# Two chained 2048-wide layers in fp32: a third Winograd level for product P5 in all but each phase's first group, where P2 stays whole; other places for the adapter rounds

## Chip, core, metric

One NeuronCore of a Trainium2 chip. The metric is the device time of one execution in microseconds, the median of several runs; the profile shows one further execution of the same program. TensorE (PE) multiplies, VectorE (DVE) adds and subtracts, ScalarE (ACT) copies from PSUM to SBUF, GpSimd (POOL) and SyncE (SP) issue DMAs.

## What is computed

The reference, cut to its core (x is 32 x 128 x 2048, all in fp32):

```python
base = einsum('bsi,oi->bso', x, weight) + bias
low = einsum('bsi,bri->bsr', x, lora_a[id0])        # rank 16, one of 8 adapters per batch
delta = einsum('bsr,bor->bso', low, lora_b[id0])
x = x + base + scale[id0][:, None, None] * delta    # first layer
x = x + einsum('bij,bkj->bik', x, weight1[id1])     # second layer: one of 16 weights per batch
```

The residual is folded into the weight: identity is added to the diagonal of W, so a layer is x (W^T + 1).

## The kernel before

**First layer.** It is Winograd's form of Strassen's product (7 products of half size in place of 8), nested. At the top level there are 7 **phases** (`PHASES`, L24): each names the quarters of x and of W whose signed sum is multiplied, where the result goes, and which products go down to the third level. A phase runs over 4 **groups** of batches, so there are 28 groups, n = 4i + g for phase i and group g. In a group the second level makes 7 products, P1 to P7, each a 512x512 piece of W with a 512x256 piece of x. A product that stays **whole** is 4 steps of 4 matmuls 128x256 (`whole`, L775). A product with a third level (**deep**) is 7 steps of 4 matmuls 128x128 (`third`, L799), on sums of its quarters that DVE makes first (`third_level`, L518: four operations of 256 elements for x, four of 512 for W) and adds up afterwards (`third_sums`, L816). Before the change P2, P3 and P4 are deep everywhere but for P2 of group 0; P1, P5, P6 and P7 are whole.

**Operands.** `total` in `a_tasks` and `w_tasks` adds up the loaded quarters of x and W (the tasks "x" and "w"), `inner` makes the second level's sums (S1 to S4 of x, T1, T2 and T4 of W; the tasks "s" and "t"), `third` the third level's ("x3" and "w3"). P5 multiplies S1 with T1, P6 S2 with T2, P3 S4 with W2, P4 A3 with T4.

**Memory.** All operands lie in one tile, `mem`. `Loads` (L112) hands its places out of pools: ten for x ("A", a group takes seven: four pieces, three sums), ten for W, six for staging ("st"), four for results ("z"). A load is issued on SP once a place is free, and the places come free as products end.

**Adapter.** Phase 1 (`LOW`, groups 4 to 7) loads all raw pieces of x and makes a @ x.T for the next group in four **rounds** (`lowrank`, L686: 32 small matmuls each, into a spare PSUM bank). Round q + 1 can start only when its staging loads have landed, and part of their places come free with round q. `lowrank_out` (L712) scales two rounds' result. In the last four phases ("final", groups 12 to 27) `add_low` (L736) makes low times b in two halves, with rows of b that `load_b` (L723) fetched on POOL's queue, and ACT copies the result (L759) to where `finish` (L840) adds it before the write to x1t in DRAM.

**Order.** Each engine works its queue off in order. PE's order is written out by hand in the loop over groups (L944 to L1067: `give` takes pairs of product and step, product 8 being P4 of the group before). DVE's order comes from `Plan` (L55): it keeps rough clocks of PE, DVE and DMA, and `fill` puts, wherever DVE's clock is behind PE's, the ready task with the smallest wanted time; `need` forces a task before the PE step that reads it. So a changed wanted time or estimated landing changes DVE's queue.

**Second layer** (L1075 on): 128 rounds of seven products each, DVE-heavy, weights streamed from DRAM. No line of it is touched.

Of the kernel before, what the change touches and what calls it, by code (L numbers as in the profile page):

```python
# [21 lines left out]
LOW = 1  # L22
KEPT = (2, 2)
PHASES = [  # L24
    ([(1, 0, 0)], [(1, 0, 0)], None, ((0, 0), (0, 1)), False, False, (2, 3, 4)),
# [3 lines left out]
        None, ((0, 1),), True, False, (2, 3, 4),  # L29
# [4 lines left out]
        (0, 1), ((1, 1), (1, 0)), False, False, (2, 3, 4),  # L34
# [4 lines left out]
        None, ((0, 1), (1, 1)), True, True, (2, 3, 4),  # L39
    ),  # L40
    ([(1, 0, 1)], [(1, 1, 0)], None, ((0, 0),), True, True, (2, 3, 4)),
# [3 lines left out]
        None, ((1, 0),), True, True, (2, 3, 4),  # L45
# [4 lines left out]
        None, ((0, 1),), True, True, (2, 3, 4),  # L50
# [61 lines left out]
class Loads:  # L112
# [13 lines left out]
    def pump(self):  # L126
        plan, full, rest = self.plan, set(), []
        for item in self.todo:
            key, pool, begin, behind, size = item
            if pool in full or not self.free[pool] or (behind and behind not in plan.did):  # L130
                full.add(pool)
                rest.append(item)
                continue
            slot = self.free[pool].pop(0)
            self.held[key] = (pool, slot)
            plan.did[key] = plan.pe
            if begin:
                begin(slot)
                plan.dma = max(plan.pe + 2.0, plan.dma) + size * 2.9
                plan.did[key] = plan.dma + 1.0  # L140
        self.todo = rest
# [20 lines left out]
def cond_resid_kernel(  # L162
# [13 lines left out]
):  # L176

# [187 lines left out]
    with tc.tile_pool(name="c0", bufs=1) as c0:  # L365
        L2 = 2 * NF

        more_w = {
            k: c0.tile([P, 3, 2, 2 * P], F32, tag=f"more_w{k}", name=f"more_w{k}") for k in (2, 3, 4)
        }  # L370
        more_a = {
            k: c0.tile([P, 3, 2, S], F32, tag=f"more_a{k}", name=f"more_a{k}") for k in (2, 3, 4)
        }

        low = c0.tile([P, B // 4, S], F32, tag="low", name="low")
        b_sel = c0.tile([P, 8, P], F32, tag="b_sel", name="b_sel")
# [3 lines left out]
        pairs_l = bank[:, 4:6], bank[:, 6:8]  # L380
        AT = {2: (0, 0), 3: (0, 1), 4: (1, 0), 1: (0, 0), 6: (0, 1), 7: (1, 0), 5: (1, 1)}
# [4 lines left out]
        def deep(n, k):  # L386

            return k in PHASES[groups[n][0]][6] and (n, k) != (0, 2)
# [4 lines left out]
                "W": (6, 0, 2, 8, 3, 5, 1, 9, 4, 7), "A": (25, 23, 28, 26, 27, 22, 21, 24, 29, 20), "z": (30, 31, 32, 33),  # L393
                "st": (36, 37, 39, 35, 34, 38), "k": (),
# [7 lines left out]
        def add_w(i, q):  # L402
# [14 lines left out]
            loads.add(("W", i, q), "W", lambda slot: load(slot, *terms[0][1:]), size=1.0)  # L417
# [96 lines left out]

        def signed(sign, dst, src):
            (add if sign > 0 else sub)(dst, dst, src)

        def third_level(work, m11, m12, m21, m22, more, of_x):  # L518

            s, u, v = (more[:, k] for k in range(3))  # L520
# [16 lines left out]
        def a_tasks(n, begin):  # L537
# [3 lines left out]
            forms = acts[n] = {k: {} for k in (2, 3, 4)}  # L541
# [4 lines left out]
            def total(q):  # L546
# [7 lines left out]
                if q == 0:  # L554
                    forms[1] = dst.rearrange("p (i n) -> p i n", i=4)
# [8 lines left out]
            def inner(k):  # L564
# [9 lines left out]
                if k < 4:  # L574
                    forms[4 + k] = dst.rearrange("p (i n) -> p i n", i=4)
# [8 lines left out]
            def third(k):  # L584
                src = slot(*{2: ("A", n, 1, 0), 3: ("S", n, 4), 4: ("A", n, 3, 0)}[k]).rearrange(
# [4 lines left out]
                    more_a[k], True,  # L590
                )

            for k, last_use, want in ((2, ("s", n, 4), 12), (3, ("s", n, 4), 32), (4, ("s", n, 1), 46)):
                if deep(n, k):
                    plan.add(
                        ("x3", n, k), begin + want, lambda k=k: third(k), last_use,
                        *([("PE", n - 1, k)] if n else []),
                    )

        def w_tasks(i, begin):  # L600
# [3 lines left out]
            forms = wts[i] = {k: {} for k in (2, 3, 4)}  # L604
# [4 lines left out]
            def total(q, f):  # L609
# [14 lines left out]
                if q == 0:  # L624
                    forms[1] = dst.rearrange("p (i n) -> p i n", i=4)
# [9 lines left out]
            def inner(k):  # L635
# [9 lines left out]
                if k < 4:  # L645
                    forms[4 + k] = dst.rearrange("p (i n) -> p i n", i=4)
# [8 lines left out]
            def third(k):  # L655
                src = view(*{2: ("W", i, 1), 3: ("W", i, 2), 4: ("T", i, 4)}[k]).rearrange(
# [7 lines left out]
            for k, last_use, want in ((2, 4, 9), (3, 3, 31), (4, 4, 45)):  # L664
                if k not in PHASES[i][6]:
                    continue
                plan.add(
                    ("w3", i, k), begin + want, lambda k=k: third(k), ("t", i, last_use),
                    *([("PE", 4 * i - 1, k)] if i else [("PE", 0, 2)] if k == 2 else []),
                )  # L670
# [15 lines left out]
        def lowrank(n, q, dst):  # L686
# [22 lines left out]
            plan.pe += 2.3  # L709
# [13 lines left out]
        def load_b(n):  # L723
            i, g = groups[n]
            r, c = PHASES[i][3][-1]
            for s in range(4):
# [3 lines left out]
                    in_=bt[ds(m, 1), c].rearrange("o r (k m) -> (o r) k m", k=8),  # L730
                )

        def low_banks(n):
            return pairs_a[1 - n % 2], pairs_l[3 * n % 2]

        def add_low(n, j):  # L736
# [3 lines left out]
            dst = low_banks(n)  # L740
            plan.pe += 1.3
            plan.need(("k", n, 0, j), ("k", n, 1, 1 - j))
            for k in range(4):
                for s in range(4):
                    nc.tensor.matmul(  # L745
                        dst[s // 2][:, s % 2, ts(k, S)], lhsT=b_sel[ts(s, RT), 4 * ((s // 2 + j) % 2) + k],
# [3 lines left out]
            low_out(n, j)  # L750

        def low_out(n, j):
            for t, src in enumerate(low_banks(n)):
# [3 lines left out]
                k = half(slot)  # L757
                for m in range(2):
                    nc.scalar.copy(k[:, ts(m, NF)], src[:, m])  # L759
# [14 lines left out]

        def whole(n, k, o):  # L775

            i = groups[n][0]
            pair = pairs_l[(3 * n + k) % 2] if k in (2, 3, 4) else pairs_a[(n + (k == 5)) % 2]
            dst = pair[:, o // 2, ts(o % 2, 2 * P)]
            if k in (2, 3, 4):  # L780
                w = mem[:, loads.slot({2: ("W", i, 1), 3: ("W", i, 2), 4: ("T", i, 4)}[k])]
                x = half(loads.slot({2: ("A", n, 1, 0), 3: ("S", n, 4), 4: ("A", n, 3, 0)}[k]))
                w, x = (v.rearrange("p (i n) -> p i n", i=4) for v in (w, x))
            else:
                w, x = wts[i][k], acts[n][k]
# [13 lines left out]
        def third(n, k, m):  # L799

            i, at = groups[n][0], 3 * n + k - 2
            pair, kept = pairs_l[at % 2], half(40 + at % 2)
            where = {2: (0, 0), 3: (0, 1), 5: (0, 1)}.get(m, (1, 0))
            dst = pair[:, where[0], ts(where[1], 2 * P)]
            w, x = wts[i][k][m], acts[n][k][m]
# [7 lines left out]
            if m in (1, 6, 7, 5):  # L813
                nc.scalar.copy(kept[:, ts((1, 6, 7, 5).index(m), 2 * P)], dst)  # L814

        def third_sums(n, k):  # L816
            at = 3 * n + k - 2
            pair, kept, z = pairs_l[at % 2], half(40 + at % 2), z_of(n, *AT[k])
            upper, c21, c22 = z[:, :NF], z[:, NF : NF + 2 * P], z[:, NF + 2 * P :]
            add(upper, upper, kept[:, :NF])  # L820
            add(upper, pair[:, 0], upper)
            add(c22, c22, kept[:, ts(2, 2 * P)])
            add(c22, c22, kept[:, ts(3, 2 * P)])
            add(c21, pair[:, 1, : 2 * P], c21)

        def ended(n, k):
# [3 lines left out]
            x, w, *last = {  # L830
                1: (("A", n, 0, 0), ("W", i, 0), 2, 3), 2: (("A", n, 1, 0), ("W", i, 1), 4),
                3: (("S", n, 4), ("W", i, 2), 2, 3), 4: (("A", n, 3, 0), ("T", i, 4), 1),
                5: (("S", n, 1), ("T", i, 1), 2), 6: (("S", n, 2), ("T", i, 2), 4),
                7: (("A", n, 2, 0), ("W", i, 3)),
            }[k]
            loads.done(x, *(("s", n, m) for m in last if (k, m) != (3, 2) and (k, m) != (3, 3)))
            if g == 3:
                loads.done(w, *(("t", i, m) for m in last))
# [24 lines left out]
        def result_tasks(n, begin):  # L863
# [10 lines left out]
            def single(k):  # L874
                if deep(n, k):
                    third_sums(n, k)
                else:
                    plain(*AT[k], pairs_l[(3 * n + k) % 2])

            plan.add(("third", n, 2), begin + 31, lambda: single(2), ("PE", n, 2))  # L880
            plan.add(("P5", n), begin + 40, both, ("PE", n, 5), ("PE", n, 6))
# [4 lines left out]
            plan.add(("third", n, 4), begin + 66, lambda: single(4), ("PE", n, 4))  # L886
# [34 lines left out]
        def give(n, *steps):  # L921

            for k, m in steps:
                of = n - 1 if k == 8 else n
                k = 4 if k == 8 else k
                if k not in (2, 3, 4):
# [7 lines left out]
        def ready(n, k):  # L934
# [3 lines left out]
            else:  # L938
                plan.need(*{
                    2: (("x", n, 1), ("w", i, 1, 1)), 3: (("s", n, 4), ("w", i, 2, 1)),  # L940
                    4: (("x", n, 3), ("t", i, 4)),
                }[k])

        for n, (i, g) in enumerate(groups):  # L944
# [10 lines left out]
            if lowering:  # L955
                plan.add(
                    ("out", n + 1, 0), begin + 33, lambda: lowrank_out(n + 1, 0, spare[:, 0, :S]),
# [3 lines left out]
                    ("out", n + 1, 1), begin + 46, lambda: lowrank_out(n + 1, 1, across[:, 0, :S]),  # L961
# [4 lines left out]
            if n:  # L966
                ready(n - 1, 4)
                plan.need(("third", n - 1, 2))
                if i == LOW:
                    plan.need(("out", n, 1))  # L970
# [6 lines left out]
            if final:  # L977
                plan.need(("P7", n - 1), ("third", n - 1, 3))
                add_low(n, 0)
                plan.fill()  # L980
            if n:
                give(n, (8, 3), (8, 4))
                ended(n - 1, 4)
            give(n, (1, 2), (1, 3))
            ended(n, 1)
            if ends:
                assert set(loads.free["W"]) == {0, 1, 2, 3}, loads.free
# [6 lines left out]
            if n == 0:  # L994
                give(n, *((2, o) for o in range(1, 5)))
            else:
                give(n, (2, 1))
            plan.need(("s", n, 1), ("t", i, 1))
            if n:
                give(n, (5, 0), (2, 2), (2, 6), (5, 1), (2, 5), (2, 7))  # L1000
            else:
                give(n, (5, 0), (5, 1))
            if lowering:
                if n:
                    plan.need(("third", n - 1, 4))
                lowrank(n + 1, 0, spare[:, 0, :S])
                plan.fill()
            if n:
# [214 lines left out]
```

## Time and profile before

| what | us |
|---|---|
| median of 3 runs (2959.79 to 2961.54) | 2960.71 |
| the profiled execution: its own time | 2960.55 |
| its span, first to last instruction | 2958.9 |
| first layer: PE from its first product to the second layer's first matmul (8.3 to 1408.3) | 1400.1 |
| second layer, from there to the end | 1550.6 |
| PE busy over the span (17,512 records, two for each matmul) | 2932.1 |
| DVE busy over the span | 2337.3 |
| DVE busy in 8.2 to 1408.3 | 893.4 |
| DVE busy in 1408.3 to the end | 1443.1 |
| ACT, POOL busy over the span | 340.5, 201.8 |

A row of the page's groups reads: line of the kernel, engine, operation, what is written from what, count, busy time and mean duration, then the idle time of the engine just before and what ended it. A line of the timeline gives start and length of a run of equal instructions, and in brackets the idle time before it with its releaser. The matmuls' lengths overlap, so a step's cost is the distance from its start to the next step's start.

### The profile page before, as it was taken

To read this page: it belongs to the slowest core of one execution; us is meant where nothing else is said; L and a number is where in the kernel's file an instruction comes from. 1 tells how busy PE (TensorE), PEld (TensorE's weight loads), DVE (VectorE), ACT (ScalarE), POOL (GpSimd) and SP (SyncE) were. 2 spreads that over 40 slices of the span, in tenths; PEclk is the share of its full clock that TensorE was granted. 3 is DMA by queue.
4 is the path that set the end of the run, shared out by engine and by line. 5 is a ranking of instruction groups with operands and counts; after the bars stand their busy time and mean duration, and the time that the engine had idled before them with its cause. 6 is when DMAs were issued, how large, how long until landed. Compare 5 with 4: busy or idle time off the path is not lost.

```text
span 2958.9 us, 43572 instructions
## 1 busy us (share of the span) xinstructions
PE 2932.1 (99%) x17512; PEld 1790.1 (60%) x17512; DVE 2337.3 (79%) x2168; ACT 340.5 (12%) x717; POOL 201.8 (7%) x323
## 2 busy tenths in 40 slices
PE   9999999999999999999999999999999999999999
PEld 8988899999989999999333333333333333333333
DVE  7457586685654745764999999999999999999997
ACT  1111111222222222222000000000000000000000
POOL 1122200111111111110000000000000000000000
PEclk9999999999999999999999999999999999999999
DMA  9498976778673635465999999999999999999995
GB/s 341 163 343 303 290 218 251 291 234 194 160 189 87 178 87 149 123 185 149 348 417 388 396 382 409 391 396 383 398 398 383 399 381 411 389 394 387 407 380 231
DMA packets 188713, 887.87 MB, mean 300 GB/s; under 512 B 21600, under 2 KB 21600, under 8 KB 122976
## 3 DMA queue, kind: packets, MB, share of 16 engines
q1 hardware_dynamic: 137616, 738.91, 63.5%
q0 software_dynamic: 32800, 113.28, 16.0%
q10 hardware_dynamic: 18096, 32.91, 3.4%
q8 instruction: 138, 2.26, 0.3%
q14 instruction: 63, 0.52, 0.0%
HBM read 754.98 MB, written 130.02 MB: 299 GB/s over the span
## 4 chain that ended last, share of the span: by engine, by line
PE 87%; DMA 5%; DVE 4%; issue 2%; SPq 0%; ACT 0%; POOL 0%; POOLq 0%; DVEq 0%; ACTq 0%
PE bank L1115 51%; PE bank L788 21%; PE bank L809 14%; DVE mem L282 2%; DMA mem<-in_xq_dram 2%; DVE mem L278 2%; DMA mem<-in_w0q_dram 1%; DMA x1t<-mem 1%; PE bank L745 1%; DMA mem<-in_w1q_dram 1%; PE bank L702 1%; DVE more_w L282 0%; SPq L444 0%; ACT mem L759 0%; DVE low L718 0%
## 5 line engine op out<-in xcount | busy, mean ns | idle before, releaser
L282 DVE TENSOR_TENSOR mem<-mem 128x2048 f32<-128x2048 f32 (+2 forms) x856 | 1494.5, 1773 | 147.9 <-DMA mem<-in_w0q_dram 44.5
L1115 PE MATMUL bank<-mem 128*64 128x512 f32 x5120 | 1122.9, 593 | 5.1 <-DVE u L278 2.9
L788 PE MATMUL bank<-mem 128*128 128x256 f32 x3616 | 835.5, 381 | 2.0 <-DVE low L718 1.6
L1115 PEld LDWEIGHTS bank<-mem 128*64 128x64 f32 x5120 | 367.8, 137 | 737.7 <-issue 696.7
L788 PEld LDWEIGHTS bank<-mem 128*128 128x128 f32 x3616 | 665.9, 191 | 82.9 <-DVE low L718 2.1
L278 DVE TENSOR_TENSOR mem<-mem 128x1024 f32<-128x1024 f32 (+2 forms) x441 | 347.5, 799 | 179.8 <-PE bank L809 75.0
L1115 PE MATMUL bank<-mem,s 128*64 128x512 f32 x2048 | 461.2, 592 | 0.0
L1115 PEld LDWEIGHTS bank<-mem,s 128*64 128x64 f32 x2048 | 147.1, 137 | 292.4 <-issue 289.2
L278 DVE TENSOR_TENSOR mem<-bank,mem 128x512 f32<-128x512 f32 (+2 forms) x195 | 127.5, 654 | 193.8 <-ACT mem L794 160.0
L809 PE MATMUL bank<-mem 128*128 128x128 f32 x1992 | 262.3, 277 | 4.3 <-ACT mem L759 4.1
L809 PEld LDWEIGHTS bank<-mem 128*128 128x128 f32 x1992 | 251.6, 192 | 17.0 <-ACT mem L759 6.2
L794 ACT COPY mem<-bank 128x512 f32<-128x512 f32 x224 | 131.5, 587 | 640.9 <-PE bank L788 635.8
L1121 ACT COPY pv<-bank 128x512 f32<-128x512 f32 x32 | 18.8, 586 | 1518.6 <-PE bank L1115 944.0
L855 POOL DMA_DIRECT2D x1t<-mem x160 | 118.1, 759 | 978.2 <-DVE mem L278 377.1
L809 PE MATMUL bank<-more_a,more_w 128*128 128x128 f32 x1328 | 171.8, 276 | 4.2 <-DVE more_w L282 3.2
L809 PEld LDWEIGHTS bank<-more_a,more_w 128*128 128x128 f32 x1328 | 166.6, 193 | 8.9 <-issue 4.7
L814 ACT COPY mem<-bank 128x256 f32<-128x256 f32 x332 | 124.4, 375 | 380.1 <-PE bank L809 373.6
L278 DVE TENSOR_TENSOR pv<-bank,pv 128x512 f32<-128x512 f32 x64 | 44.2, 691 | 66.7 <-PE bank L1115 65.4
L278 DVE TENSOR_TENSOR mem<-mem,ident 128x1024 f32<-128x1024 f32 (+1 forms) x84 | 85.4, 1029 | 11.1 <-DMA mem<-in_w1q_dram 10.8
L809 PE MATMUL bank<-more_a,mem 128*128 128x128 f32 x664 | 89.2, 277 | 0.0
L809 PEld LDWEIGHTS bank<-more_a,mem 128*128 128x128 f32 x664 | 84.9, 191 | 4.7
L809 PE MATMUL bank<-mem,more_w 128*128 128x128 f32 x664 | 87.7, 275 | 0.0
(43 smaller groups left out, 686.9 us busy)
## 6 DMA issues: line engine op xcount, KB each, us to landing
mem<-in_w1q_dram SPq DMA_DIRECT2D x512, 1024.0 KB, 10.9
mem<-in_xq_dram SPq DMA_DIRECT2D x192, 512.0 KB, 7.2
x1t<-mem POOLq DMA_DIRECT2D x160, 512.0 KB, 7.8
mem<-in_w0q_dram SPq DMA_DIRECT2D x88, 512.0 KB, 10.2
mem<-x1t SPq DMA_DIRECT2D x80, 512.0 KB, 9.0
out_dram<-res ACTq DMA_DIRECT2D x124, 256.0 KB, 7.4
mem<-in_at_dram POOLq DMA_DIRECT2D x64, 128.0 KB, 5.5
xsum<-mem POOLq DMA_DIRECT2D x16, 512.0 KB, 7.3
```

What stands on the lines that cost most here:

```text
L278: nc.vector.tensor_tensor(dst, a, b, ALU.add)
L282: nc.vector.tensor_tensor(dst, a, b, ALU.subtract)
L702: nc.tensor.matmul(dst[ts(2 * r + s, RT)], lhsT=a_sel[:, 2 * r + s, k, i], rhs=raw[r, k][:, i, s], start=(h == k == i == 0), stop=(h == k ...
L745: nc.tensor.matmul(dst[s // 2][:, s % 2, ts(k, S)], lhsT=b_sel[ts(s, RT), 4 * ((s // 2 + j) % 2) + k], rhs=low[ts(s, RT), 4 * r + g], star ...
L788: nc.tensor.matmul(dst, lhsT=w[:, m, ts(o, P)], rhs=x[:, m], start=(k < 6 and o % 2 == 0 and m == 0), stop=(m == 3), skip_group_check=True,)
L794: nc.scalar.copy(by_block(z_of(n, *AT[k]))[:, o - 1 : o + 1], pair[:, o // 2].rearrange("p (k t m) -> p k t m", k=2, t=2),)
L809: nc.tensor.matmul(dst[:, ts(o, P)], lhsT=w[:, f, ts(o, P)], rhs=x[:, f], start=(m in (1, 2) and o == f == 0), stop=(f == 1), skip_group_c ...
L814: nc.scalar.copy(kept[:, ts((1, 6, 7, 5).index(m), 2 * P)], dst)
L855: nc.gpsimd.dma_start(out=of_x1t(rc, g, t, j), in_=src.rearrange("p (s x) -> p s x", s=2), accum_op=ALU.add if adding else ALU.bypass,)
L1115: nc.tensor.matmul(dst[ts(j, M)], lhsT=xts[pair, k4 // 2][k][:, j, k4 % 2 * 2 + i], rhs=w1s[n][k][:, j, i], start=(k4 == 0 and i == 0), st ...
L1121: nc.scalar.copy(pv[:, 0], dst)
```

## The change

P5 is added to every phase's list of deep products; `deep` now leaves P2 and P5 whole in each phase's first group (g = 0). The other edits: x's third-level sums share three buffers that go round (`more_x`) in place of one per product; one of the ten "A" places (half 28 of `mem`) and one new buffer become W's third-level sums for P5; rows of b are held by halves and fetched twice per final group; the third-level sums of W for P2 and P5 wait for the first group's whole product, since they overwrite part of W; P2's and P5's steps are interleaved in a new order; the four rounds of a @ x.T stand elsewhere; the waits for `lowrank_out` move; `Plan` takes a load to land 4 us later than it did. In the second layer nothing changes.

```diff
-    ([(1, 0, 0)], [(1, 0, 0)], None, ((0, 0), (0, 1)), False, False, (2, 3, 4)),
+    ([(1, 0, 0)], [(1, 0, 0)], None, ((0, 0), (0, 1)), False, False, (2, 3, 4, 5)),
...
-                plan.did[key] = plan.dma + 1.0
+                plan.did[key] = plan.dma + 5.0
...
-        more_w = {
-            k: c0.tile([P, 3, 2, 2 * P], F32, tag=f"more_w{k}", name=f"more_w{k}") for k in (2, 3, 4)
-        }
-        more_a = {
-            k: c0.tile([P, 3, 2, S], F32, tag=f"more_a{k}", name=f"more_a{k}") for k in (2, 3, 4)
-        }
+        w_c0 = c0.tile([P, 10, 2, 2 * P], F32, tag="more_w", name="more_w")
+        w_mem = mem[:, 14, :L2].rearrange("p (k i n) -> p k i n", k=2, i=2)
+        more_w = {k: [w_c0[:, 3 * m + n] for n in range(3)] for m, k in enumerate((2, 3, 4))}
+        more_w[5] = [w_mem[:, 0], w_mem[:, 1], w_c0[:, 9]]
+        more_x = c0.tile([P, 3, 3, 2, S], F32, tag="more_x", name="more_x")
+        kept_5 = c0.tile([P, 2 * P], F32, tag="kept_5", name="kept_5")
...
-        b_sel = c0.tile([P, 8, P], F32, tag="b_sel", name="b_sel")
+        b_sel = c0.tile([P, 4, P], F32, tag="b_sel", name="b_sel")
...
+        SMALL = (2, 5, 3, 4)
...
-            return k in PHASES[groups[n][0]][6] and (n, k) != (0, 2)
+            i, g = groups[n]
+            return k in PHASES[i][6] and (g > 0 or k in (3, 4))
...
-                "W": (6, 0, 2, 8, 3, 5, 1, 9, 4, 7), "A": (25, 23, 28, 26, 27, 22, 21, 24, 29, 20), "z": (30, 31, 32, 33),
+                "W": (6, 0, 1, 8, 2, 5, 3, 9, 4, 7), "A": (20, 21, 27, 29, 24, 25, 26, 22, 23), "z": (30, 31, 32, 33),
...
-            loads.add(("W", i, q), "W", lambda slot: load(slot, *terms[0][1:]), size=1.0)
+            loads.add(
+                ("W", i, q), "W", lambda slot: load(slot, *terms[0][1:]), size=1.0,
+                behind=("A", 4 * i - 3 + q, 3, 0) if i == LOW + 1 and q < 3 else None,
+            )
...
-            for k, last_use, want in ((2, ("s", n, 4), 12), (3, ("s", n, 4), 32), (4, ("s", n, 1), 46)):
+            for k, last_use, want in ((2, 4, 12), (5, 2, 12.5), (3, 4, 32), (4, 1, 46)):
                 if deep(n, k):
+                    before = turn(n, k) - 3
+                    before = [("PE", before // 4, SMALL[before % 4])] if before >= 0 else []
...
-            for k, last_use, want in ((2, 4, 9), (3, 3, 31), (4, 4, 45)):
-                if k not in PHASES[i][6]:
-                    continue
-                plan.add(
-                    ("w3", i, k), begin + want, lambda k=k: third(k), ("t", i, last_use),
-                    *([("PE", 4 * i - 1, k)] if i else [("PE", 0, 2)] if k == 2 else []),
-                )
+            for k, last_use, want in ((2, 4, 50), (5, 2, 51), (3, 3, 31), (4, 4, 45)):
+                if k in PHASES[i][6]:
+                    before = ("PE", 4 * i - 1, k) if deep(4 * i, k) else ("PE", 4 * i, k)
...
...
+                upper, third_one, fifth = kept_of(n, k)
+                to = {1: upper[:, : 2 * P], 6: upper[:, 2 * P :], 7: third_one, 5: fifth}[m]
+                nc.scalar.copy(to, dst)
+            elif m == 4 and k == 5:
+                nc.scalar.copy(z_of(n, 1, 1)[:, NF : NF + 2 * P], dst)
...
+            if k != 5:
+                add(upper, upper, first)
+                add(c22, c22, third_one)
+                add(c21, pair[:, 1, : 2 * P], c21)
             add(upper, pair[:, 0], upper)
+            add(c22, c22, fifth)
...
-            plan.add(("P5", n), begin + 40, both, ("PE", n, 5), ("PE", n, 6))
+            plan.add(("third", n, 5), begin + 26.5, lambda: single(5), ("PE", n, 5))
+            plan.add(("P5", n), begin + 40, both, ("third", n, 5), ("PE", n, 6))
...
-                if i == LOW:
-                    plan.need(("out", n, 1))
                 give(n, (8, 1))
...
                 add_low(n, 0)
+                load_b(n, 1)
...
+            if i == LOW:
+                plan.need(("out", n, 1))
             give(n, (1, 2), (1, 3))
...
-                give(n, (5, 0), (2, 2), (2, 6), (5, 1), (2, 5), (2, 7))
...
-                lowrank(n + 1, 0, spare[:, 0, :S])
...
-                give(n, (5, 2), (2, 3), (2, 4), (5, 3))
...
-                lowrank(n + 1, 1, spare[:, 0, :S])
+                give(n, (2, 1), (2, 2))
+                ready(n, 5)
+                give(n, (5, 1), (2, 6))
+                if not deep(n, 2):
+                    give(n, (5, 2), (2, 3))
+                if lowering:
+                    plan.need(("third", n - 1, 4))
+                    lowrank(n + 1, 0, spare[:, 0, :S])
+                    plan.fill()
+                give(n, *[(5, 2)] * deep(n, 2), (2, 5), (5, 6), *[(5, 3)] * (not deep(n, 2)))
+                give(n, (2, 7), (5, 5), *[(2, 3)] * deep(n, 2), (5, 7), (2, 4))
+                give(n, *[(5, 3)] * deep(n, 2), (5, 4))
...
-            give(n, *((6, o) for o in range(4)))
+            give(n, (6, 0))
+            if lowering:
+                lowrank(n + 1, 1, spare[:, 0, :S])
+                plan.fill()
+            give(n, *((6, o) for o in range(1, 4)))
...
-            if lowering:
-                lowrank(n + 1, 2, across[:, 0, :S])
...
-                give(n, (7, 0), (3, 6), (3, 5), (7, 1))
+                give(n, (7, 0))
                 if lowering:
-                    lowrank(n + 1, 3, across[:, 0, :S])
+                    plan.need(("third", n, 5))
+                    lowrank(n + 1, 2, across[:, 1, :S])
                     plan.fill()
-                give(n, (3, 7), (7, 2), (3, 3), (3, 4), (7, 3))
+                give(n, (3, 6), (3, 5), (7, 1), (3, 7), (7, 2), (3, 3), (3, 4))
+                if lowering:
+                    lowrank(n + 1, 3, across[:, 1, :S])
+                    plan.fill()
+                give(n, (7, 3))
```

## Prediction

> **What bounds the kernel.** I read the table of windows first, split where the second layer's first matmul starts, then the page's chain.
>
> ```profile
> 8.20:1408.30 1400.10, 1385.05 (x10312) 1268.98 (x10312) 893.40 (x1296) 320.42 (x684) 196.53 (x310) 1.00 0.68 207
> 1408.30:2958.90 1550.60, 1540.67 (x7169) 514.93 (x7168) 1443.10 (x871) 18.76 (x32) 1.72 (x2) 1.00 0.97 385
> PE 87%; DMA 5%; DVE 4%; issue 2%; SPq 0%; ACT 0%; POOL 0%; POOLq 0%; DVEq 0%; ACTq 0%
> ```
>
> Behind each stretch's length stand the busy times of PE, PEld, DVE, ACT and POOL, the granted clock and the DMA share. In the first layer PE works 1385 of 1400 us and DVE 893: PE sets the end, and time changes only with PE's steps or its waits. The second layer, 1550.6 us, keeps its instructions and, by the order of the changed program, its first loads wait for the same products; I leave it as it is.
>
> The timeline of PE gives the steps' prices:
>
> ```profile
> 58.29 1.06 PE L809 MATMUL bank<-more_a,mem 128*128 128x128 f32 x8
> 59.19 1.06 PE L809 MATMUL bank<-mem,more_w 128*128 128x128 f32 x8
> 60.08 3.62 PE L788 MATMUL bank<-mem 128*128 128x256 f32 x16
> 63.53 1.05 PE L809 MATMUL bank<-mem 128*128 128x128 f32 x8
> ```
>
> From start to start a deep step takes 0.89 us (median 0.893 over the layer), a whole step 3.45/2 = 1.726. The waits of PE in this layer:
>
> ```profile
> PE bank L702 <- DMA mem<-in_xq_dram: 4.9, 5, 2.0
> PE bank L809 <- ACT mem L759: 4.1, 3, 3.0
> PE bank L809 <- DVE more_w L282: 3.2, 1, 3.2
> PE bank L788 <- DVE low L718: 1.6, 3, 0.7
> PE bank L809 <- DVE more_a L282: 1.0, 1, 1.0
> PE bank L788 <- DVE mem L278: 0.4, 1, 0.4
> ```
>
> They cost more than their sum. Adding up by how much each step exceeds its usual length gives 24.7 us: 1.2 at 38 us; 4.1 in a @ x.T at the end of group 3; 9.8 in group 4, the first of phase 1; 2.7 in groups 5 to 7; 6.9 in the final groups (4.9 of it at group 16). The rest is half clock:
>
> ```profile
> 217.87 1.05 PE L809 MATMUL bank<-mem 128*128 128x128 f32 x8
> 222.11 2.04 PE L809 MATMUL bank<-more_a,more_w 128*128 128x128 f32 x8 [3.19 <-DVE more_w L282]
> 223.95 2.55 PE L788 MATMUL bank<-mem 128*128 128x256 f32 x8
> 226.34 1.05 PE L809 MATMUL bank<-more_a,more_w 128*128 128x128 f32 x8
> 221.90:225.30 3.40, 3.19 (x12) 2.95 (x13) 3.23 (x7) 0.37 (x1) 0.00 (x0) 0.50 1.02 417
> ```
>
> After 3.19 us idle the clock is 0.50 for 3.4 us; the deep step takes 1.84 in place of 0.89, the whole one 2.39 in place of 1.73: 1.6 us on top.
>
> **PE's steps.** Before, 3 x 28 - 1 = 83 products are deep; after, P3 and P4 in 28 groups and P2 and P5 in 21: 98. Fifteen more (21 P5 gained, 6 P2 lost). A whole product is 4 x 1.726 = 6.90 us, a deep one 7 x 0.893 = 6.25: 15 x 0.65 = **-9.8 us**. [...] The row says 0.52 of a whole step, over 581 steps with weight loads: I take the row.
>
> **DVE.** A deep P5 adds four operations of 0.42 (more_a, 128x256) and sums of 0.69 and 0.42: 2.8 us a group; each phase adds four of 0.69 for W; six P2 give back about 3 each. In 650:700 DVE is busy 28.7 of 50 us, so this lies beside PE where its place in the queue is early enough. In the changed order of a usual group, DVE makes P2's and P5's x sums behind P7's, P3's and one result's additions; they are queued to end some 11 us after the last P7 step starts, and the first step that reads one starts at 19. Cover 8 us; each us beyond costs PE one.
>
> **ACT.** P5 goes from two copies of 0.59 to five of 0.375, and between a copied step and the step that overwrites its bank there are now at least two deep steps, 1.8 us. Before, P4 has a single step (0.89) there and PE shows no wait for L814. Nothing.
>
> **POOL and DMA.** 64 more b fetches, four per final group, about 1 us each on POOL (0.5 busy, 0.5 issue; POOL is busy some 20 of 200 us). The second half's fetch waits for add_low's matmuls, and behind it on POOL stands the write of result (0,1), later by some 5 us; its reader, the copy after the second add_low, comes 20 us later. Nothing, 0 to 3. Nine x places in place of ten: a group's last x pieces load after P1 and P2 (16 and 26 us in) and are read 10 us and more later, at 7.2 us per landing (the page's x row). Nothing, 0 to 4.
>
> **Waits that go.** At 38 us PE waited for P3's x sums because DVE did the scale table first; now the sums come first: 1.2 to 0. The half of `low` that held PE at group starts (1.6) is asked for four steps and more later: 0. The rounds of a @ x.T: each needs loads issued when the round before has freed its staging. The distances were 5.2, 6.9 and 7.0 us of PE work, now 10.7, 8.7 and 7.9 (6.9 between the first two in group 4), against 7.2 to land. I take 4.1 to 0.5 in group 3, and 2.7 to 1.5 in groups 5 to 7.
>
> **The wait that stays: group 4.** Here DVE is full (44.3 of 50 us in 200:250). The fourth round has moved from mid P3 to just before P7's last step, so DVE work moves behind it too: its x sum, four `low` operations, and the last W sum, whose staging load is issued only after the round. In the trace of before:
>
> ```profile
> 195.61 1.63 SPq L423 DMA_DIRECT2D mem<-in_w0q_dram  x2
> 202.60 1.23 DVE L278 TENSOR_TENSOR mem<-mem 128x1024 f32<-128x1024 f32 x1 [0.39 <-DMA mem<-in_w0q_dram]
> ```
>
> Some 7 us from the first issue to DVE's release. Then DVE's queue: that W sum 1.2, P7 1.2, P3's additions 2.6, four x sums 4.9, P4's additions 2.6, T1 2.3 = 14.8, so T1 is there 21.5 us after the round. PE's first P5 step comes after 5 whole steps, 7 deep and 2 whole: 7 x 1.73 + 7 x 0.89 = 18.4. Wait 3.2, plus 1.6 of half clock as at 222 us. [...] From T1 to `low` DVE has T2, T4, T3 6.9, two x third levels 3.4, three of W 8.2, two x roundings 4.9, P2's addition 1.2, `low` 1.6 = 26.2; PE to its reader, P3's second step, 10 whole steps, two rounds at 1.88, one deep step and the half clock: 17.3 + 3.8 + 0.9 + 1.6 = 23.6. Wait 2.6. Group 4: 9.8 to 7.4. Between: 4 if the load lands faster, 13 if it lands like the page's 10.2 us for W.
>
> **Final groups.** Group 16 waited 3.0 us for ACT's L759 copy, itself held by a write to x1t. In the new order a W piece is loaded ahead of that stretch and the other result's writes go later; I take 4.9 to 1.5, and 2.0 for the other groups' (unchanged). Bounds 0.5 and 7.
>
> **Sum.** Waits after: 0 + 0.5 + 7.4 + 1.5 + 3.5 = 12.9; for 21 groups of new interleaving that no row shows I add 2: 15. Change -9.8 - 24.7 + 15 = -19.5; on the profiled execution's own 2960.55 (span 2958.9 and 1.65 around it; the median of the runs is 2960.71) **2941 us**.
>
> **Rivals.**
> - The waits only move (chance 0.2): DVE and DMA around phase 1 are as full as before, each gap closed opens the next, and 21 to 25 us of waits stay. For it: the load-bound DVE queue of group 4. Against: the rounds' wider distances. Only PE's steps remain: 2960.6 - 9.8 = 2951.
> - Slower (0.06): x's late places. S4's place now comes free only when P3 of the group before ends, so S4 and P2's third level start behind it, in every group. If x loads or DVE's backlog eat the 8 us of cover, PE waits in all 27 later groups. It decides from 9.8 + 9.7 = 19.5 us, 0.7 a group; with 1 us, 27 more than my sum: 2968. Against: DVE's idle third.
> - The level does not pay (0.03): deep steps spaced wider when P2 and P5 alternate, by 0.06 us or more each; 147 P5 steps x 0.067 eat the 9.8: 2951. Against: all 581 deep steps show one spacing whatever stands beside them.
>
> **Chances.** 0.71 for the forecast (own range 2934 to 2948). What a measurement here can tell from no change is 0.2%, 5.9 us: faster means below 2954.8. The first and third rivals lie on the faster side, with about a fifth of them within; faster 0.87, within 0.06, slower 0.07. The range, with 4 to 13 at group 4, 0.5 to 7 in the final groups and the moving-waits case: 2931 to 2953.
>
> **What would show it.** Deep matmul records 4648 to 5488, whole ones 3616 to 3136; PE's first layer 1380 us; no wait of L809 for more_w at group 4's P2, but one of L806 for DVE's `mem` sum at its P5, followed by clock 0.50; waits for in_xq_dram under 2 us. Wrong if PE shows waits at each group's P2 or P5, or if ACT's copies hold PE there.

## The result, and the profile after

| | before | after |
|---|---|---|
| median of 6 runs each, us | 2960.25 (2958.6 to 2964.58) | 2938.43 (2936.55 to 2939.1) |
| ratio after / before, 95% interval | | 0.9923 [0.991, 0.9936] |
| profiled execution: own time, span, us | 2960.55, 2958.9 | 2939.1, 2937.5 |
| first layer of the profile, us | 1400.1 | 1378.3 |
| steps' excess in it (waits, half clock), us | 24.7 | 12.6 |

The kernel is 0.77% faster, 21.8 us by the medians. The forecast of 2941 missed by 2.6 us. First the windows of the changed kernel, split where the second layer's first matmul starts (length of the stretch, then busy times of PE, PEld, DVE, ACT and POOL, the granted clock, DMA's share), then the first line of the page's chain:

```profile
8.20:1386.50 1378.30, 1367.48 (x10674) 1266.89 (x10674) 934.96 (x1401) 325.38 (x723) 230.34 (x374) 1.00 0.70 210
1386.50:2937.50 1551.00, 1540.47 (x7169) 508.59 (x7168) 1442.82 (x871) 18.75 (x32) 1.71 (x2) 1.00 0.97 385
PE 91%; DMA 3%; DVE 3%; issue 2%; SPq 0%; POOL 0%; ACT 0%; POOLq 0%; DVEq 0%; ACTq 0%
```

All of the gain lies in the first layer: 21.8 us there, while the second takes 1551.0 in place of 1550.6. DVE does 42 us more in the first layer (935 for 893) and PE still ends it. The waits of PE up to 1420 us, by what ended them (us in total, times, longest):

```profile
PE bank L717 <- DVE mem L279: 3.0, 2, 1.8
...
PE bank L806 <- DVE mem L283: 2.3, 1, 2.3
PE bank L826 <- DVE low L733: 2.3, 1, 2.3
...
PE bank L717 <- DMA mem<-in_xq_dram: 1.5, 1, 1.5
...
```

L806 is a whole step, L826 a deep one, L717 a round of a @ x.T. The 4.9 us in front of the rounds for x's loads have become 1.5, the waits for `more_w` and for half of `low` at group starts are gone. New is the first row: in groups 5 and 6 the first round waits for additions of DVE. PE's timeline shows four of these places:

```profile
213.95 5.45 PE L806 MATMUL bank<-mem 128*128 128x256 f32 x24 [2.34 <-DVE mem L283]
...
238.84 1.16 PE L826 MATMUL bank<-mem 128*128 128x128 f32 x8 [2.30 <-DVE low L733]
...
244.44 1.08 PE L717 MATMUL bank<-mem 128*32 128x128 f32 x32 [1.49 <-DMA mem<-in_xq_dram]
...
275.41 1.84 PE L717 MATMUL bank<-mem 128*32 128x128 f32 x58 [1.23 <-DVE mem L279]
```

The first is P5's first step in group 4, waiting for T1; the second is P3's second step there, waiting for `low`; the next is in the middle of the third round, still in group 4, waiting for a load of x; the last is the first round in group 5. The clock did not fall after any of them: the trace grants 1.00 throughout the first layer, where the kernel before had four stretches at 0.50.

### The profile page after: what moved, and what is told of

It is laid out like the page before. It is cut to its first block, busy times and chain, and to the rows that moved or that the text cites. A ratio compares the mean times of both kernels' runs of the same rounds, so it can differ in the third digit from the quotient of the medians.

```text
span 2937.5 us, 44863 instructions
## 1 busy us (share of the span) xinstructions
PE 2913.5 (99%) x17872; PEld 1780.8 (61%) x17872; DVE 2378.7 (81%) x2274; ACT 345.4 (12%) x756; POOL 235.6 (8%) x387
## 4 chain that ended last, share of the span: by engine, by line
PE 91%; DMA 3%; DVE 3%; issue 2%; SPq 0%; POOL 0%; ACT 0%; POOLq 0%; DVEq 0%; ACTq 0%
PE bank L1140 51%; PE bank L806 20%; PE bank L826 18%; DVE mem L279 1%; DVE mem L283 1%; PE bank L760 1%; DMA x1t<-mem 1%; DMA mem<-in_w1q_dram 1%; PE bank L717 1%; DMA mem<-in_w0q_dram 1%; DMA mem<-in_xq_dram 0%; DMA id_sb<-in_id_dram 0%; DVE low L733 0%; DVE more_x L283 0%; SPq L429 0%
## 5 line engine op out<-in xcount | busy, mean ns | idle before, releaser
L283 DVE TENSOR_TENSOR mem<-mem 128x2048 f32<-128x2048 f32 (+3 forms) x892 | 1514.3, 1725 | 208.6 <-PE bank L826 101.3
L806 PE MATMUL bank<-mem 128*128 128x256 f32 x3136 | 715.4, 380 | 4.8 <-DVE mem L283 2.3
L806 PEld LDWEIGHTS bank<-mem 128*128 128x128 f32 x3136 | 578.7, 190 | 77.8 <-DVE mem L283 2.7
L279 DVE TENSOR_TENSOR mem<-mem 128x256 f32<-128x256 f32 (+2 forms) x423 | 331.5, 810 | 74.8 <-ACT mem L812 38.7
L826 PE MATMUL bank<-mem 128*128 128x128 f32 x2352 | 301.3, 276 | 2.6 <-DVE low L733 2.3
L826 PEld LDWEIGHTS bank<-mem 128*128 128x128 f32 x2352 | 289.3, 192 | 11.9 <-DVE low L733 2.5
L279 DVE TENSOR_TENSOR mem<-bank,mem 128x256 f32<-128x256 f32 (+2 forms) x210 | 135.5, 676 | 169.1 <-PE bank L826 92.6
L826 PE MATMUL bank<-more_x,more_w 128*128 128x128 f32 x1232 | 158.6, 275 | 0.0
L826 PEld LDWEIGHTS bank<-more_x,more_w 128*128 128x128 f32 x1232 | 151.7, 192 | 3.5 <-issue 0.8
L826 PE MATMUL bank<-more_x,mem 128*128 128x128 f32 x1120 | 146.1, 276 | 0.0
L826 PEld LDWEIGHTS bank<-more_x,mem 128*128 128x128 f32 x1120 | 136.6, 192 | 3.3
L826 PE MATMUL bank<-mem,more_w 128*128 128x128 f32 x784 | 103.7, 275 | 0.0
```

The source lines that it names most:

```text
L279: nc.vector.tensor_tensor(dst, a, b, ALU.add)
L283: nc.vector.tensor_tensor(dst, a, b, ALU.subtract)
L806: nc.tensor.matmul(dst, lhsT=w[:, m, ts(o, P)], rhs=x[:, m], start=(k < 6 and o % 2 == 0 and m == 0), stop=(m == 3), skip_group_check=True,)
L826: nc.tensor.matmul(dst[:, ts(o, P)], lhsT=w[:, f, ts(o, P)], rhs=x[:, f], start=(m in (1, 2) and o == f == 0), stop=(f == 1), skip_group_c ...
```

## Experiments

Each kernel was timed beside the kernel before on the same chip. Since that kernel's median differed from chip to chip (2961.0, 2963.5, 2961.5), ratios are what to compare. "First layer" and "excess" are read from the profile as in the table above: PE's time from the first product to the second layer, and the sum of what steps take beyond their usual length. "Second layer" is the rest of the profiled execution. No line of it differs between these kernels, and it still varies by 8 us, so a gain in the first layer is not yet a gain of the whole.

| run | ratio [95% interval] | first layer, us | excess, us | second layer, us |
|---|---|---|---|---|
| before | 1 | 1400.1 | 24.7 | 1550.6 |
| after | 0.9923 [0.991, 0.9936] | 1378.3 | 12.6 | 1551.0 |
| p5_whole | 0.9949 [0.9936, 0.9963] | 1385.3 | 6.7 | 1548.8 |
| rounds_alone | 0.9996 [0.9988, 1.0004] | 1396.0 | 20.6 | 1554.7 |
| nine_places | 0.9988 [0.998, 0.9997] | 1398.4 | 23.9 | 1548.1 |
| p2_first | 0.9928 [0.9914, 0.9941] | 1378.1 | 16.8 | 1552.0 |
| rounds_p2 | 0.9995 [0.9986, 1.0004] | 1398.1 | 19.3 | 1556.4 |
| p5_not01 | 0.9916 [0.9902, 0.9929] | 1374.2 | 5.3 | 1553.1 |
| p5_not1 | 0.9927 [0.9913, 0.994] | 1380.4 | 13.0 | 1549.7 |
| landing_1 | 0.9941 [0.9928, 0.9955] | 1384.5 | 19.5 | 1551.3 |
| rounds_p2_land | 1.0004 [0.9995, 1.0013] | 1399.3 | 20.6 | 1553.1 |
| rounds_back | 0.995 [0.9937, 0.9964] | 1386.7 | 21.8 | 1549.8 |
| late_p2 | 0.9916 [0.9903, 0.993] | 1375.5 | 9.9 | 1550.8 |
| late_p25 | 0.991 [0.9895, 0.9925] | 1377.0 | 14.7 | 1550.9 |

**P5's third level undone.** In the changed kernel:

```diff
-    ([(1, 0, 0)], [(1, 0, 0)], None, ((0, 0), (0, 1)), False, False, (2, 3, 4, 5)),
+    ([(1, 0, 0)], [(1, 0, 0)], None, ((0, 0), (0, 1)), False, False, (2, 3, 4)),
...
```

and so in all seven phases.

> The changed kernel with P5 whole in every group (its third level undone; P2 whole in each phase's first group, and rounds, needs and places as changed). It has 21 products P5 more as four whole steps in place of seven deep ones: 21 x (4 x 1.726 - 7 x 0.893) = 21 x 0.65 = 13.7 us more of steps. Theory (the third level of P5 pays its steps in full, and the waits went for the other reasons): 2938.4 + 13.7 = 2952, and 1 to 3 us less than that if the wait at P5's first step in group 4 came with P5's deep form. Rival (the third level does not pay; all of the gain is from waits): 2938 to 2941.

Measured: 2945.58 us, 0.9949. The step sum is there (first layer less excess: 1378.6 for 1365.7, so 12.9 us), but the waits fall with it from 12.6 to 6.7. Neither theory named that size: P5's level is worth 7 us net, 12.9 of steps less 5.9 of waits that come with it. Of the gain of 22 us, 15 stand without it, although P2 in six groups is slower there than before.

**The rounds alone, in the kernel before.**

```diff
-            if lowering:
-                lowrank(n + 1, 1, spare[:, 0, :S])
-                plan.fill()
...
-            give(n, *((6, o) for o in range(4)))
+            give(n, (6, 0))
+            if lowering:
+                lowrank(n + 1, 1, spare[:, 0, :S])
+                plan.fill()
+            give(n, *((6, o) for o in range(1, 4)))
```

and likewise for the third and fourth round and `low`'s second half.

> The kernel before with the four a @ x.T rounds at their new steps, the other half of the bank and the need for low's second half two steps later; no third level for P5, all places as before. Theory (the rounds' waits were real and go): group 3's 4.1 us fall to about 0.5, groups 5 to 7's 2.7 us to about 1.5, and a part of group 4's 9.8: 2952 to 2956. Rival (waits only move to the next need): 2959.5 to 2961.

Measured: 2959.3 us, 0.9996, no change that can be told. In the rounds the reasoning holds: group 3's 4.1 us are gone, and groups 5 to 7 show no wait at all. But group 4 goes from 9.8 to 14.5. Its waits (us in total, times, longest):

```profile
PE bank L788 <- DVE mem L282: 6.2, 1, 6.2
...
PE bank L809 <- DVE low L718: 2.0, 1, 2.0
```

PE comes to P5's first step earlier and waits there 6.2 us for T1, then 2.0 for `low`. The first layer is 4.1 us shorter all the same, and the second takes it back: it is 4.1 us longer. SP issues its next loads of weights from 1422.31 us on, behind a write to x1t (1409.16 in the kernel before), DVE waits for such a load, and PE for DVE; the eight records behind that wait take 3.63 us, where eight such records of the changed kernel take 1.92 at a clock of 1.00 (from 1427.19 us on):

```profile
1422.31 31.51 SPq L312 DMA_DIRECT2D mem<-in_w1q_dram  x17
```

```profile
1437.04 3.63 PE L1118 MATMUL bank<-mem,s 128*64 128x512 f32 x8 [3.99 <-DVE mem L282]
```

So the rival (waits only move) holds for this part taken alone: in part they move to group 4, in part beyond the layer. Which place in memory held the loads is not shown.

**Nine places for x, in the kernel before.**

```diff
-"A": (25, 23, 28, 26, 27, 22, 21, 24, 29, 20)
+"A": (25, 23, 26, 27, 22, 21, 24, 29, 20)
```

> The kernel before with nine places for A and S in place of ten (half 28 left out), nothing else changed. Theory (the tenth place was not what x waited for): 2959.5 to 2962. Rival (x's late places: the load of a group must then wait for S4's place, free only after P3): 1 us or more in each of 27 groups, about 2987.

In this kernel S4 of the last group lies where the second layer's first load of x goes, so P3 of group 27 is made from other data and the result is wrong there; the 27 groups before it are as in the kernel before. Measured: 2957.77 us, 0.9988, first layer 1398.4 us, a little faster than the theory's range and far from the rival's 2987. The tenth place was worth nothing here. The changed kernel uses its nine places in another order, but there too no wait for x's sums stands in the usual groups, so the slow rival of the prediction falls.

**P2 deep in the first groups too, in the changed kernel.**

```diff
-            return k in PHASES[i][6] and (g > 0 or k in (3, 4))
+            return k in PHASES[i][6] and (g > 0 or k in (3, 4) or k == 2 and n > 0)
```

> The changed kernel with P2 in the deep form also in the first group of the phases after the first (six products: 6 x 0.65 = 3.9 us fewer of steps), and with it the need of group 4's P2 for the third-level sums of W. Theory (the exception is for the first low phase, where VectorE is late): group 4's wait grows by about the third-level sums of W for P2, some 4 us, and the sum is 2936 to 2940; without a wait elsewhere. Rival (no wait grows, steps alone): 2934.5.

Measured: 2940.11 us, 0.9928. Group 4's excess grows from 7.0 to 12.6 us (a wait of 4.1 for `more_w`, and 10.2 us of half clock around it), which is more than the 3.9 of steps; the first layer comes out even, 1378.1. So leaving P2 whole there is about free in steps and waits together.

**The rounds and the whole P2, in the kernel before.** As rounds_alone, and

```diff
-            return k in PHASES[groups[n][0]][6] and (n, k) != (0, 2)
+            return k in PHASES[groups[n][0]][6] and (groups[n][1] > 0 or k in (3, 4))
...
-            for k, last_use, want in ((2, 4, 9), (3, 3, 31), (4, 4, 45)):
+            for k, last_use, want in ((2, 4, 50), (3, 3, 31), (4, 4, 45)):
...
```

> The kernel before with the four a @ x.T rounds at their new steps and P2 whole in each phase's first group (its third-level sums of W wanted at 50 of the group in place of 9); no third level for P5, all places, wants and the landing estimate as before. Steps: six products P2 more as whole ones, 6 x 0.65 = 3.9 us more. Theory (rounds alone gave nothing because group 4 waits for VectorE all the same, at P2 and at P5's first step; with the third-level sums of W for P2 taken out of VectorE's queue there, that wait goes): waits 24.7 to about 10, so 2961 + 3.9 - 14.7 = 2950. Rival (the other places, wants and landing estimate are what took the waits away): 2961 to 2965.

Measured: 0.9995; the first layer is 2.0 us shorter than before, the second 5.8 longer. The theory falls: 15.3 us of excess stay in group 4 (of 19.3), now at P2's and P5's first steps and at the second round. With the third-level sums of W out of the way, something else holds group 4.

**P5 whole in phases 0 and 1, in the changed kernel.** The diff is p5_whole's, in the first two phases only.

> The changed kernel with P5 whole in groups 0 to 7 (phases 0 and 1) and in the deep form in the later phases' groups as changed: six products more as whole ones, 3.9 us more of steps. Theory (P5's third-level sums on VectorE are what the groups 4 to 6 wait for: 12.6 us of waits in the first layer with them, 6.7 with no P5 deep at all): waits 5 to 6 us less, so 2936.5. Rival (the waits come from something else in groups 4 to 6): 2942.

Measured: 0.9916, first layer 1374.2 us, excess 5.3. In the windows of its first layer PE is busy for all but 4 us:

```profile
8.50:1382.70 1374.20, 1370.28 (x10528) 1265.49 (x10528) 916.94 (x1357) 321.85 (x705) 231.09 (x374) 1.00 0.69 211
```

The theory holds in the first layer: between 195 and 360 us PE waits for no sum of DVE any more, only for loads of x (2.3 us). Leaving P5's level out of these two phases costs 3.2 us of steps by the profile (3.9 by the count) and takes 7.3 off the excess. The second layer gives back 2.1 of that.

**P5 whole in phase 1 only.**

> The changed kernel with P5 whole in groups 4 to 7 only: three products more as whole ones, 2.0 us more of steps. Theory (the waits in front of round 0 in groups 5 and 6, 3.0 us, are from P5's third-level sums of the same groups; group 4's waits, 5 us, are from those of group 3 and stay): 2937 to 2938. Rival (group 4's waits are from the sums of its own phase, which then go too): 2933 to 2935; other rival (no wait goes): 2940.4.

Measured: 0.9927. The profile shows the expected in part. The first rounds in groups 5 and 6 no longer wait for DVE, and T1 is still late in group 4:

```profile
215.32 6.92 PE L806 MATMUL bank<-mem 128*128 128x256 f32 x23 [2.77 <-DVE mem L283]
```

But the third rounds, in groups 4 to 6, now wait more for x's loads (3.7 us in four waits, for 1.5 in one), so nothing is won: the excess is 13.0. Only with phase 0 whole as well, where T1 is in time for group 4, did the sum fall.

**The landing estimate undone, in the changed kernel.**

```diff
-                plan.did[key] = plan.dma + 5.0
+                plan.did[key] = plan.dma + 1.0
```

> The changed kernel with the planner's estimate of a load's landing at 1.0 us after its transfer, as before, in place of 5.0. Theory (a sum planned too early stands in VectorE's order ahead of work that could run, and VectorE waits for the load): 2939 to 2943. Rival (the estimate moves nothing on the path): 2938 to 2939.

Measured: 0.9941, so 0.0018 or 5.3 us slower than the changed kernel, 6.2 in the first layer of the profile; the two intervals overlap a little. The change's own order of DVE before group 4, then this kernel's:

```profile
190.75 1.23 DVE L283 TENSOR_TENSOR mem<-mem 128x1024 f32<-128x1024 f32 x1 [5.99 <-DMA mem<-in_w0q_dram]
...
211.61 6.94 DVE L283 TENSOR_TENSOR mem<-mem 128x2048 f32<-128x2048 f32 x3
```

```profile
193.42 1.23 DVE L283 TENSOR_TENSOR mem<-mem 128x1024 f32<-128x1024 f32 x1 [8.52 <-DMA mem<-in_w0q_dram]
```

With the short estimate DVE stands 8.5 us before W's sums and twice 1.7 later, with other work queued behind; with the long one 6.0 and then no more than 0.7 at a time. T1, the first of the line of three sums 128x2048, starts at 211.6 with the long estimate and at 216.3 with the short one, and PE waits 5.5 us for it, with 6.8 us of half clock after. Three more waits, 3.7 us, come in `add_low` in groups 15 and 19.

**Rounds, whole P2 and landing, in the kernel before.** As rounds_p2, with the estimate at 5.0.

> The kernel before with the rounds at their new steps, P2 whole in each phase's first group, and the planner's landing estimate at 5.0 us; no third level for P5, wants and places as before. The same without the landing estimate gave a ratio of 0.9995, the changed kernel with P5 whole (which has the other wants and places too) 0.9949. Theory (the landing estimate is the part that was missing: sums no longer stand at the head of VectorE's queue while their load is under way): ratio 0.995 to 0.997, 2946 to 2951. Rival (the wants, and the W loads held behind x's, are needed as well): 0.999 to 1.000, 2958 to 2961.

Measured: 1.0004. The rival holds. In group 4 the rounds wait 7.8 us for x's loads, in four waits, and 17.1 us of the layer run at half clock. Three parts of the change that each look like the cause, put together, give nothing; the changed kernel with P5 whole, which differs from this run in the wanted times, the order of P2's and P5's steps, the places and buffers, the halved rows of b and the held W loads, is 16 us faster, 14 of them in the first layer. SP's DMA issues around group 4, in this run:

```profile
197.71 0.99 SPq L411 DMA_DIRECT2D mem<-in_w0q_dram  x2
...
199.24 1.67 SPq L411 DMA_DIRECT2D mem<-in_w0q_dram  x2
201.01 8.01 SPq L444 DMA_DIRECT2D mem<-in_xq_dram  x4
211.19 3.74 SPq L411 DMA_DIRECT2D mem<-in_w0q_dram  x2
```

and with the changed kernel's order (p5_whole):

```profile
196.89 28.23 SPq L450 DMA_DIRECT2D mem<-in_xq_dram  x11
225.18 0.90 SPq L414 DMA_DIRECT2D mem<-in_w0q_dram  x2
```

L411 (L414) loads the first piece of a W quarter of the next phase. In the first, six of these transfers of 512 KB go out between 197 and 215 us among x's loads. In the second none goes before 225, since the change holds three such loads back until the next groups' x pieces are under way (the `behind` in `add_w`). From issue to landing, x's loads issued in 204:219 take (KB each, median us), in this run and in p5_whole:

```profile
mem<-in_xq_dram SPq DMA_DIRECT2D x4, 512.0 KB, 20.5
```

```profile
mem<-in_xq_dram SPq DMA_DIRECT2D x3, 512.0 KB, 7.8
```

The other kernels fall on the same two sides: 16.0 us before the change, 18.2 in rounds_alone and 20.5 in rounds_p2, which hold nothing back, and 7.0 to 9.2 in the changed kernel, rounds_back, landing_1 and p5_not01. The DMA engines move 345 GB/s in 195:250 of this run, so six transfers are, as an estimate, 6 x 524288 / 345000 = 9.1 us of all of them, most of the 12.7 us between the two medians. That the hold shortens the landing of x's loads and so takes the waits out of group 4 is argued from these rows, since the two sides differ in the other edits too; holding the loads alone was not tried.

**The rounds at their old steps, in the changed kernel.** The diff is that of rounds_alone the other way round, with the banks and needs as changed.

> The changed kernel with the second, third and fourth a @ x.T round at the steps where they stood before (the halves of the banks, needs and all else as changed). Theory (each round needs loads issued when the round before has freed its staging, so the old distances bring the old waits back): 4 us in group 3 and 1 to 2 us more in groups 5 to 7, less what group 4 then waits less: ratio 0.9935 to 0.9945, 2941 to 2944. Rival (waits only move from the rounds to group 4): 0.992 to 0.993, 2937 to 2940.

Measured: 2946.74 us, 0.995, 8 us slower than the changed kernel. The old waits come back, larger than expected (us in total, times, longest):

```profile
PE bank L717 <- DMA mem<-in_xq_dram: 13.2, 8, 5.0
```

So the same edit is worth 4 us of the first layer and nothing in total in the old surroundings, and 8 us in the new ones.

**P2, then P2 and P5, deep in the later first groups.** Both start from p5_not01:

```diff
-            return k in PHASES[i][6] and (g > 0 or k in (3, 4))
+            return k in PHASES[i][6] and (g > 0 or k in (3, 4) or k == 2 and n > 4)
```

and for the second `or n > 4` for the last term; the sums of W are wanted 41 earlier where they are needed by a first group.

> P5 whole in groups 0 to 7 as in the run p5_not01 (ratio 0.9916), and P2 deep in the first groups of the phases from group 8 on, with the third-level sums of W for it wanted early: five products fewer as whole ones, 3.3 us fewer of steps. Theory (only group 4 lacks room on VectorE; in the later first groups it has some): waits grow by 0 to 1.5 us, ratio 0.9905 to 0.9911, 2932.5 to 2934.5. Rival (each first group waits for its W sums, about what the steps give): 0.9915 to 0.992.

> As late_p2, with P5 deep as well in the first groups from group 8 on: ten products fewer as whole ones than in the run p5_not01, 6.5 us fewer of steps. Theory (room on VectorE in the later first groups): waits grow by 1 to 3 us, ratio 0.990 to 0.9905, 2931 to 2933. Rival (the third-level sums of W for P2 and P5, 5.5 us on VectorE in a row, are late in each of five groups): 0.9915 to 0.993.

Measured: 0.9916 and 0.991, in the profile first layers of 1375.5 and 1377.0, not shorter than p5_not01's 1374.2. Steps fell by 3 and 7 us and the excess rose by 4.6 and 9.4: in late_p25 the final groups wait 4.8 us for ACT's copies of `low` times b, and the rounds for x's loads 6.5. The rival holds; steps taken off PE came back as waits.

No version beats the changed kernel beyond doubt. p5_not01's first layer is 4.1 us shorter in the profile, but its second is 2.1 us longer, and the two intervals overlap widely.

## Why the prediction was right

**Steps, -9.8: right.** The first layer less its excess went from 1375.4 to 1365.7 us, -9.7. The page's row of whole steps counts what was forecast:

```profile
L806 PE MATMUL bank<-mem 128*128 128x256 f32 x3136 | 715.4, 380 | 4.8 <-DVE mem L283 2.3
```

The four kinds of deep step sum to 5488 records, and a deep step still takes 0.893 us, a whole one 1.729 (medians from start to start): 0.52 of a whole step, as in the row that the prediction took.

**Waits, 24.7 to 15: right in sum, with luck in its parts.**

| place | forecast, us | measured, us |
|---|---|---|
| start | 0 | 0 |
| group 3 | 0.5 | 0 |
| group 4 | 7.4 | 7.0 |
| groups 5 to 7 | 1.5 | 3.3 |
| final groups | 3.5 | 2.3 |
| allowance for new interleaving | 2 | - |
| sum | 14.9 | 12.6 |

- Group 4: both named waits stand where they were forecast, and for the reason given. T1 is there 20.9 us after the round (forecast 21.5), PE would be at P5's first step 18.5 after it (18.4), and waits 2.3 us (3.2); `low` holds P3's second step for 2.3 (2.6). Two terms are wrong and nearly cancel: the 1.6 of half clock did not come, and 1.8 that was not forecast did, a load of x in the third round.
- Groups 5 to 7: the step "I take 4.1 to 0.5 in group 3, and 2.7 to 1.5 in groups 5 to 7" looked at loads only. No wait for loads is left there. But in groups 5 and 6 the first round needs P4's additions of the group before, and DVE comes late with them: 3.3 us.
- The DVE part, "this lies beside PE", is the step that failed. It was read from a usual group, and in usual groups it holds: in 650:700 of the changed kernel DVE is busy 31.6 of 50 us and PE all 50. Its terms add up to 60 us more of DVE, where 42 were measured. Even so, P5's level costs some 7 us of waits around groups 4 to 6 (p5_not01), about half of the 13.7 that its steps give in all.
- That 12.6 lies near 14.9 is luck in part: terms of 6.3 us did not come (the half clock, the allowance, the loads in groups 5 to 7 and 1.2 of the final groups), against 5.1 us that no term named.
- Nothing was charged for the landing estimate: it is worth 5 us in the changed kernel. Its effect was inside the forecast, since group 4 was worked out from the changed program's DVE order, but its share was not named.
- The rounds' gain was written as a term of its own. It is none: nothing in total in the old surroundings, 8 us in the new.

**Rivals.** The slow one (x's late places) was refuted by nine_places. That waits only move did not come true for the whole change, but it describes six of the partial versions, in whole or in part: both rounds_p2 runs, rounds_alone, p5_not1, late_p2 and late_p25. With the level's steps among them, the 686 deep steps are still spaced 0.893 us apart in the median, so the third falls too.

**Open:** which of the remaining edits (the held W loads, the wanted times, P2's and P5's order, the places) takes the 14 us of excess out between rounds_p2_land and p5_whole. So the sum of steps and waits is shown, but not the share of each edit in the waits.

## What to carry to other kernels

Where several queues are full in one place, the worth of an edit depends on the others: sum the waits of the place with all edits in, from the changed order, rather than crediting each edit with the wait that it seems to remove. Adding up the excess of each step over its usual length gives both terms apart (steps and waits), and each experiment can then be checked on both. Look at the stretch behind as well: what is gained in front of it can be lost there. P5's sums went on an engine with an idle third: in a usual stretch, where DVE is now busy 31.6 of 50 us, PE waited for none of them, but around groups 4 to 6 (DVE busy 48.6 of 55 us in 195:250) they cost some 7 us. So look for the stretch where that engine has no idle third, and spare just that stretch.

## What was not expected of the hardware

In these traces the length of PE's wait does not alone tell whether the clock drops; where the idle time falls counts too. While PE works, the kernel before has five stretches at a clock of 0.50, each 3.413 us long; they begin at 184.32, 221.86, 238.93, 826.02 and 1512.10 us, so 37.55, 17.07, 587.09 and 686.08 us apart: 11, 5, 172 and 201 times 3.4133 us. The changed kernel has one, at 1489.89 us, and a second at 2937.14, when PE's work is done, 1447.25 us or 424 times 3.4133 behind it. If this grid runs through the whole trace, which is an estimate from these starts, 374 steps before 1489.89 is 213.30. There it cuts the wait of 2.34 us in two, and the clock stays at 1.00. In p5_not1 2.41 of the 2.77 us, at the same step, lie in the 3.42 us up to 216.33, and in rounds_alone all of the 2.01 us in the 3.41 up to 249.27; there the clock is 0.50 in the next 3.41. The stretches with these waits, for the latter two runs with the stretch that follows:

```profile
209.89:213.30 3.41, 1.72 (x8) 1.16 (x7) 3.41 (x6) 0.00 (x0) 1.05 (x2) 1.00 1.02 419
```

```profile
212.91:216.33 3.42, 1.01 (x5) 0.91 (x6) 3.38 (x3) 0.00 (x0) 1.05 (x2) 1.00 1.03 422
216.33:219.74 3.41, 3.41 (x10) 2.70 (x9) 3.38 (x2) 0.00 (x0) 0.00 (x0) 0.50 1.02 418
```

```profile
245.86:249.27 3.41, 1.40 (x11) 1.18 (x10) 3.30 (x7) 0.96 (x2) 1.74 (x3) 1.00 1.00 359
249.27:252.68 3.41, 3.41 (x13) 3.05 (x13) 1.00 (x1) 0.00 (x0) 1.61 (x3) 0.50 1.04 285
```

PE is idle for 1.69 us of the first, 2.41 and 2.01 of the other two. In the kernel before, laid out on this grid from 8.2 us to PE's last matmul, PE is idle for 1.93, 2.93, 2.05, 2.62 and 2.94 us in the steps of the grid just ahead of the five stretches at 0.50, and in the changed kernel for 2.41 us ahead of the one. In every other grid step at 1.00 of these two traces PE idles for at most 1.78 us, and 1.00 stays. So a forecast of half clock from the length of a wait alone, like the prediction's 1.6 us, can go either way: 1.00 stayed after a wait of 2.34 us, and 0.50 followed one of 2.01.
